# Two macaron blocks on one core: rings of q and k for the first two head groups moved into the pool beside the feed-forward, and chunk 1's q and k prepared there

## The chip, the cores and the metric

The kernel runs on one core of a Trainium2 chip. Its five engines work side by side, each on its own queue of instructions in program order: TensorE (PE; PEld is its loading of weights), VectorE (DVE), ScalarE (ACT), GpSimd (POOL) and SyncE (SP), which here issues nearly all DMA transfers. Engines wait for one another through semaphores. The metric is the time of one execution on the device in microseconds (us); lower is better. Times of the kernel before are the median of three runs and one execution with the profiler on.

## What is computed

One sequence of S = 2048 tokens with E = 256 features passes through two blocks. Each block is feed-forward (halved), attention, feed-forward (halved), each on a layernorm of x and added to x:

```python
x = x + 0.5 * _L0_ffn_ref(_layernorm(x), w_gate_up, w_proj)      # f0
x = x + _L0_attn_ref(_layernorm(x), W_qkv, W_o)                  # layer 0
x = x + 0.5 * _L0_ffn_ref(_layernorm(x), w_gate_up, w_proj)      # f1
x = x + 0.5 * _L1_ffn_ref(_layernorm(x), w_gate, w_up, w_down)   # f2
x = x + _L1_attn_ref(_layernorm(x), Wq, bq, Wk, bk, Wv, bv, Wo, bo)   # layer 1
x = x + 0.5 * _L1_ffn_ref(_layernorm(x), w_gate, w_up, w_down)   # f3
```

Both attentions are causal with 16 heads of 16 features. Layer 0 adds a slope per head times the distance (ALiBi); layer 1 adds biases and turns q and k by a rotary embedding (rope). The layer 0 feed-forward has ternary weights, silu(gate) times up over 1024 hidden features, and an RMS norm ahead of the second product. The layer 1 feed-forward keeps, of each four hidden features, the two that are largest in size.

## The kernel before

x stays in SBUF transposed (features on partitions) in four chunks of 512 tokens. A feed-forward goes chunk by chunk, eight steps f each: gate and up matmuls (pg, L306 and L281), silu on ACT (L317), the product on DVE (L318), and, per chunk, the second matmul (po, L361 and L292), part of which runs during the next chunk's steps. For the last chunk po stands alone at the end. Layernorms of chunks already done run piece by piece in between (`pull`); `pending[c]` counts those of chunk c still under way, and `ready(c)` draws them to their end.

Instructions on PE, ACT, DVE and POOL stay in the order in which the Python code issues them. Work is interleaved by generators: each `yield` hands the turn back. `attention(layer, following)` is such a generator. Its first value is the generator `first()`, which prepares chunk 0 beside the end of the feed-forward ahead of the attention: `beside0` and `beside1` begin it once the room is free, and `go_on` draws one step of it per f in the second half of the third chunk and in the fourth, two per f in the fourth chunk if the weights of layer 1 are loaded, as they are ahead of layer 1. `attend()` draws what is left of it after the feed-forward, and then the rest of the attention. What `first()` uses lies in pool `ka`, opened beside the feed-forward on the other side of SBUF. All else of the attention lies in pools `kv` and `at` (L640 to L642), opened when the feed-forward's pool is closed, so that their tiles take over its room and wait for its last readers.

Preparation of a chunk c:

- `prep_qk(c, what)` (L533 on): two pairs of matmuls (pp, L548; four instructions each, one step per pair). In layer 0 ACT casts the first bf16 piece (L556) and DVE subtracts it (L557). In layer 1 ACT adds the bias (L559); two DMAs copy the halves of dn swapped into sw (L568); a DVE multiply by the cosine (L583), a POOL multiply by the sine (L587) and a DVE add (L589) do the rope, and a cast and a subtraction (L593) give the first piece. Two more pieces follow on ACT (L595) and POOL (L596). The three pieces, which make up an fp32 value, are written to scratch in DRAM, dk or dq, with six DMAs (L601). The pieces' tiles have one buffer each; dn has two in layer 0 and one in layer 1; sw and cs have one.
- `prep_v(c)` (L607 on): two steps of eight matmuls (pv, L613), then copies into va.

`load(n, kc)` reads back the k of chunk kc for group n (four heads; n = 4 c + g), and q of group n once: one DMA of 384 KB from dk or dq (L655) and one of constant rows (L660) for each. The tiles are rings in `kv`: four of k of the group's own chunk (kd), five of k of earlier chunks (ko), four of q. SP issues these in order with all else on it.

Scores are computed twice. First for the maxima: `mx_unit` makes, for each of four heads, a score matmul (pq, L686), a mask matmul (L694), and a DVE reduce out of PSUM (mx, L697); the scores take turns in three PSUM buffers (`ps_one`), which pp, pv and others share. `mx_end` makes the negated maximum of a group in three pieces (neg, L704 and L709), `mx_turn` turns it (ptm, L719; qx on ACT, L727) and three DMAs put it into q's tile as rows (L729). Then, for every block of 128 keys, `st_pair` makes the transposed scores (pst, L748, mask L756), ACT the exponential (pT, L768) and PE the product with v (pav, L783); DVE and POOL divide (L804 to L809), and the output matmul (L824) follows.

At the attention's start there are seven units of maxima ahead of the first exponential: the four of group 0 (`maxima[-1]`, widths 128 to 512 tokens), and three of group 1. Between them `step()` draws the preparation of chunk 1 from `preps`, one step per unit in layer 0, two in layer 1:

```python
load_to(-1)
preps.extend((prep_qk(1, "k"), prep_qk(1, "q"), prep_v(1)))
for unit in maxima[-1]:
    mx_next(unit, (0, 1, 2, 3))
    for _ in range(1 + layer):
        step()
```

`load_to(i)` issues the loads of all units due by slot i; `need(...)` draws `preps` on until a piece that is wanted is there. The last unit of group 1 stands between score matmuls of the first exponential.

## Time and profile before

| what | value |
|---|---|
| median of 3 runs | 1911.72 us (1908.17, 1911.72, 1911.8) |
| profiled execution | 1911.92 us |
| its span | 1910.1 us |
| mean granted PE clock | 0.971 |
| PE busy | 1728.1 us, 90% |
| DVE busy | 1354.6 us, 71% |
| ACT busy | 892.9 us, 47% |
| POOL busy | 415.3 us, 22% |
| chain that ended last | PE 70%, DVE 18%, ACT 3%, issue 3%, POOL 3%, DMA 1% |

The span is the stretch from the first to the last instruction that the profiler recorded; the time of the execution is 1.8 us longer. The chain is found by going back from the last instruction to what released it, and so on; an engine's share there says how much of the span hung on it. The granted clock is the share of full speed that PE was allowed. In timelines the bracket at the end of a row gives how long the engine had been idle before it, and whose end released it.

### The profile page before, as it was taken

The numbers are of one execution on the slowest core, as the hardware profiler recorded it, in microseconds if no ns is written. First come the engines' busy times: TensorE is split into PE (matmuls) and PEld (weight loads), VectorE is DVE, ScalarE is ACT, GpSimd is POOL, SyncE is SP. The second block draws the span as 40 slices with busy tenths as digits, with TensorE's granted clock in tenths as the row PEclk, the third lists the DMA queues.
The fourth block names the chain that finished last, engine by engine and source line by source line (L and its number), as shares of the span: only waits on it lengthen the run. The fifth ranks groups of instructions, "written<-read, shape, count | busy, mean of one in ns | idle before, by whom it ended". The sixth has DMA issues, their size and how long they took to land.

```text
span 1910.1 us, 27066 instructions
## 1 busy us (share of the span) xinstructions
PE 1728.1 (90%) x10684; PEld 743.0 (39%) x10684; DVE 1354.6 (71%) x2400; ACT 892.9 (47%) x1158; POOL 415.3 (22%) x386
## 2 busy tenths in 40 slices
PE   5699788999999999888999995889999999998999
PEld 1234343443444443333434442434334444433443
DVE  7867368787788884467666674878877888825665
ACT  4244143555556667433442222545555556673221
POOL 3456321110000000246532332212101000004100
PEclk9799899999999999989999997999999999999999
DMA  4001143312211000200000025313112210000000
GB/s 132 1 1 61 52 130 83 103 47 79 88 56 47 28 28 1 75 1 0 1 12 0 11 89 157 106 55 115 53 46 73 84 44 27 18 2 0 11 11 22
DMA packets 50512, 93.11 MB, mean 49 GB/s; under 512 B 5425, under 2 KB 33073, under 8 KB 50129
## 3 DMA queue, kind: packets, MB, share of 16 engines
q1 hardware_dynamic: 49296, 89.28, 15.3%
q10 hardware_dynamic: 1088, 2.10, 0.3%
q8 instruction: 84, 1.38, 0.3%
q14 instruction: 44, 0.35, 0.1%
HBM read 59.51 MB, written 27.26 MB: 45 GB/s over the span
## 4 chain that ended last, share of the span: by engine, by line
PE 70%; DVE 18%; ACT 3%; issue 3%; POOL 3%; DMA 1%; SPq 0%; DVEq 0%; ACTq 0%; POOLq 0%
PE pav L783 14%; PE pst L748 11%; PE pq L686 10%; PE pg_f L281 8%; DVE mx L697 8%; PE pg_f L306 6%; PE po_f L292 6%; PE po_f L361 4%; PE pp_q L548 2%; PE pp_k L548 2%; PE pwo L824 2%; PE pv L613 1%; PE pst L756 1%; PE pq L694 1%; DVE h_f L329 1%
## 5 line engine op out<-in xcount | busy, mean ns | idle before, releaser
L697 DVE TENSOR_REDUCE mx<-pq 128x1 f32<-128x512 f32 (+3 forms) x1280 | 697.1, 602 | 145.8 <-PE pq L694 81.5
L768 ACT ACTIVATE pT<-pst 128x1024 f32<-128x1024 f32 (+3 forms) x616 | 536.4, 897 | 332.4 <-PE pst L748 171.5
L686 PE MATMUL pq<-k,q 105*128 105x512 bf16 (+7 forms) x1280 | 386.6, 350 | 72.7 <-DVE mx L697 49.0
L748 PE MATMUL pst<-q,k 99*128 99x512 bf16 (+7 forms) x1280 | 355.8, 352 | 10.4 <-ACT pT L768 6.6
L783 PE MATMUL pav<-pT,va 128*32 128x256 f32 (+1 forms) x4608 | 324.3, 377 | 5.5 <-DVE yt L804 5.0
L281 PE MATMUL pg_f<-xn,wgu 128*128 128x512 f32 x512 | 229.1, 598 | 11.9 <-DVE hr_f L318 11.8
L809 POOL TENSOR_TENSOR zt<-yt,rd 128x64 f32<-128x64 f32 x128 | 41.3, 322 | 811.4 <-DVE rd L808 807.0
L748 PEld LDWEIGHTS <-k 105*128 105x128 bf16 (+1 forms) x1280 | 111.1, 98 | 230.0 <-issue 165.9
L686 PEld LDWEIGHTS <-q 105*128 105x128 bf16 (+1 forms) x1280 | 123.3, 99 | 146.6 <-issue 45.2
L783 PEld LDWEIGHTS pav<-pT,va 128*32 128x32 f32 x4608 | 106.2, 108 | 189.5 <-issue 134.8
L306 PE MATMUL pg_f<-xn,wgu 128*128 128x512 bf16 x512 | 154.8, 410 | 19.1 <-DVE wgu L170 6.8
L317 ACT ACTIVATE sl_f<-pg_f 128x512 f32<-128x512 f32 x128 | 75.9, 593 | 172.2 <-PE pg_f L281 97.3
L281 PEld LDWEIGHTS pg_f<-xn,wgu 128*128 128x128 f32 x512 | 97.0, 191 | 138.9 <-issue 114.5
L306 PEld LDWEIGHTS <-wgu 128*128 128x128 bf16 x768 | 77.2, 101 | 162.6 <-issue 69.0
L340 POOL TENSOR_TENSOR ss_f<-ss_f,sq_f 128x512 f32<-128x512 f32 x56 | 90.6, 1617 | 112.4 <-ACT sq_f L339 107.9
L292 PE MATMUL po_f<-h_f,wd 128*128 128x512 f32 x256 | 112.1, 592 | 0.0
L694 PE MATMUL pq<-mask_qk,ident_b 128*128 128x128 bf16 x512 | 106.2, 224 | 0.0
L756 PE MATMUL pst<-mask_kq,ident_b 128*128 128x128 bf16 x512 | 102.8, 221 | 0.0
L318 DVE TENSOR_TENSOR h_f<-sl_f,pg_f 128x512 f32<-128x512 f32 x64 | 43.6, 681 | 78.7 <-ACT sl_f L317 78.5
L804 DVE STREAM_TRANSPOSE yt<-pav 128x128 f32<-128x128 f32 x128 | 39.9, 311 | 78.1 <-PE pav L783 78.1
L306 PE MATMUL pg_f<-xm_f,wgu 128*128 128x512 bf16 x256 | 84.4, 412 | 11.9 <-DVE xm_f L238 11.9
L318 DVE TENSOR_TENSOR hr_f<-sl_f,pg_f 128x512 f32<-128x512 f32 x64 | 43.7, 683 | 64.0 <-ACT sl_f L317 63.9
(132 smaller groups left out, 1787.3 us busy)
## 6 DMA issues: line engine op xcount, KB each, us to landing
k<-dk SPq DMA_DIRECT2D x80, 384.0 KB
dk<-p_k SPq DMA_DIRECT2D x48, 256.0 KB
dq<-p_q SPq DMA_DIRECT2D x48, 256.0 KB
q<-dq SPq DMA_DIRECT2D x32, 384.0 KB
x<-in_xT ACTq DMA_DIRECT2D x4, 512.0 KB
raw<-in_w_gu SPq DMA_DIRECT2D x8, 256.0 KB
wgu<-in_w_gu SPq DMA_DIRECT2D x1, 2048.0 KB
cs_k<-in_cos_sin SPq DMA_DIRECT2D x4, 512.0 KB
```

Source lines behind the costliest of these rows:

```text
L281: nc.tensor.matmul(pg[:, half, :], lhsT=wgu[:, dc, half * F + f * P : half * F + (f + 1) * P], rhs=xn[:, dc, :], start=dc == 0, stop=dc == ...
L292: nc.tensor.matmul(po, lhsT=w[:, f, dc * P : (dc + 1) * P], rhs=h[:, f, :], start=f == 0, stop=f == FC - 1,)
L306: nc.tensor.matmul(pg[:, half, :], lhsT=wgu0[:, dc, half * F + f * P : half * F + (f + 1) * P], rhs=xp[part][:, dc, :], start=part == 0 an ...
L318: nc.vector.tensor_tensor(to, sl, pg[:, 1, :], ALU.mult)
L340: nc.gpsimd.tensor_tensor(ss, ss, sq, ALU.add)
L686: nc.tensor.matmul(pq, lhsT=qs[n][0:rows, hh, t * P : (t + 1) * P], rhs=ks[n, kc][0:rows, hh, 0:w], start=True, stop=kc < c,)
L694: nc.tensor.matmul(pq[:, w - P : w], lhsT=ident_b, rhs=mask_qk, start=False, stop=True)
L697: nc.vector.tensor_reduce(mxs[n][:, t, hh, kc : kc + 1], pq, AX.X, ALU.max)
L748: nc.tensor.matmul(ps[i][:, lo:CH], lhsT=ks[n, kc][0:rows, hh, t * P : (t + 1) * P], rhs=qs[n][0:rows, hh, lo:CH], start=True, stop=kc < c,)
L756: nc.tensor.matmul(ps[i][:, lo : lo + P], lhsT=ident_b, rhs=mask_kq, start=False, stop=True)
L768: nc.scalar.activation(pT[:, :, lo:CH], pair[:, :, lo:CH], AF.Exp, scale=0.25)
L783: nc.tensor.matmul(acc[hh * SLOT : (hh + 1) * SLOT, a:b], lhsT=va[kc][:, t, v0 : v0 + SLOT], rhs=pTs[hh // 2][:, hh % 2, a:b], start=kb == ...
```

## The change

The rings are split by group. Groups whose number modulo 4 is 0 or 1 have their k of the own chunk and their q in pool `ka`, two buffers each; groups 2 and 3 have theirs in `kv`, two buffers each; all k of earlier chunks stay in `kv`, five buffers. Before `kv` is open, `ring` can only give `ka`. `first()` now also issues the loads of groups 0 and 1 for chunk 0 (after q and after v of chunk 0 are prepared), then notes "first" as done, waits until the layernorm of chunk 1 has been asked for (and, while `kv` isn't open, until it is finished), and goes on with k and q of chunk 1. What of this is not done when the feed-forward ends is drawn by `step()` in the attention, with v of chunk 1 behind it. `go_on` draws two steps per f in the fourth chunk ahead of layer 0 as well, and ahead of layer 1 already in the second half of the third; in the maxima's loop there is one step per unit in either layer. The memsets of va of chunks 1 to 3 are issued together when `kv` opens, and no longer by each chunk's preparation of k.

```diff
     def layernorm(c, name):
 
         pending[c] += 1
+        asked.add(name)
...
-    def attention(layer, following):
+    def attention(layer, before, following):
...
                 ready(c)
-                if what == "k" and c > 0:
-                    nc.gpsimd.memset(va[c], 1.0)
...
-            yield first()
-            kv = st.enter_context(tc.tile_pool(name=f"kv{layer}", bufs=1))
-            ap = st.enter_context(tc.tile_pool(name=f"at{layer}", bufs=2))
-            va += [values(kv, c) for c in range(1, NCH)]
...
+            pools = [ka]
 
             qs = {}
             ks = {}
+
+            def ring(n, other=False):
+
+                return pools[0 if other or n % 4 > 1 else -1]
...
-                need("k", kc)
-                ks[n, kc] = kv.tile(
-                    [P, 4, CH], BF16, tag="kd" if kc == c else "ko", bufs=4 if kc == c else 5,
+                ks[n, kc] = ring(n, kc < c).tile(
+                    [P, 4, CH], BF16, tag="kd" if kc == c else "ko", bufs=2 if kc == c else 5,
                     name=f"k{layer}_{n}_{kc}",
                 )
...
                 if n not in qs:
-                    need("q", c)
-                    qs[n] = kv.tile([P, 4, CH], BF16, tag="q", bufs=4, name=f"q{layer}_{n}")
+                    qs[n] = ring(n).tile([P, 4, CH], BF16, tag="q", bufs=2, name=f"q{layer}_{n}")
                     stack(qs[n], "q", c, a["q_rows"][g])
+
+            def first():
+                nc.gpsimd.memset(va[0], 1.0)
+                yield
+                for work in (prep_qk(0, "k"), prep_qk(0, "q")):
+                    yield from work
+                load(0, 0)
+                yield from prep_v(0)
+                load(1, 0)
+                done.add("first")
+                while f"after_{before}_1" not in asked or len(pools) == 1 and pending[1]:
+                    yield
+                for work in (prep_qk(1, "k"), prep_qk(1, "q")):
+                    yield from work
+
+            beginning = first()
+            yield beginning, done
+            kv = st.enter_context(tc.tile_pool(name=f"kv{layer}", bufs=1))
+            ap = st.enter_context(tc.tile_pool(name=f"at{layer}", bufs=2))
+            pools.insert(0, kv)
+            va += [values(kv, c) for c in range(1, NCH)]
+            for c in range(1, NCH):
+                nc.gpsimd.memset(va[c], 1.0)
...
                 while uses and uses[0][1] <= slot:
-                    load(*uses.popleft()[0])
+                    (n, kc), _ = uses.popleft()
+                    if (n, kc) not in ks:
+                        need("k", kc)
+                        need("q", n // G)
+                        load(n, kc)
 
             load_to(-1)
-            preps.extend((prep_qk(1, "k"), prep_qk(1, "q"), prep_v(1)))
+            preps.extend((beginning, prep_v(1)))
             for unit in maxima[-1]:
                 mx_next(unit, (0, 1, 2, 3))
-                for _ in range(1 + layer):
-                    step()
+                step()
...
         if at == NCH - 1 or at == NCH - 2 and f >= FC // 2:
             next(begun[1], None)
-            if w1 and at == NCH - 1:
+            if w1 or at == NCH - 1:
                 next(begun[1], None)
...
     def attend():
-        att, first = begun
-        for _ in first:
-            pass
+        att, first, done = begun
+        while "first" not in done:
+            next(first)
         next(att, None)
         begun.clear()
```

More of the change, by code (lines that the diff above doesn't have):

```diff
@@ L185, in macaron_kernel @@
     pending = [0] * NCH
+    asked = set()
     def draw(work):
@@ L631, in prep_v @@
                     yield
-            def first():
-                nc.gpsimd.memset(va[0], 1.0)
-                yield
-                for work in (prep_qk(0, "k"), prep_qk(0, "q"), prep_v(0)):
-                    yield from work
-            yield first()
-            kv = st.enter_context(tc.tile_pool(name=f"kv{layer}", bufs=1))
-            ap = st.enter_context(tc.tile_pool(name=f"at{layer}", bufs=2))
-            va += [values(kv, c) for c in range(1, NCH)]
-            acc = ps_acc(f"pav{layer}")
-            zts = {}
-            zs = {}
+            pools = [ka]
             qs = {}
             ks = {}
+            def ring(n, other=False):
+                return pools[0 if other or n % 4 > 1 else -1]
             def load(n, kc):
@@ L668, in load @@
                 if n not in qs:
-                    need("q", c)
-                    qs[n] = kv.tile([P, 4, CH], BF16, tag="q", bufs=4, name=f"q{layer}_{n}")
+                    qs[n] = ring(n).tile([P, 4, CH], BF16, tag="q", bufs=2, name=f"q{layer}_{n}")
                     stack(qs[n], "q", c, a["q_rows"][g])
+            def first():
[19 more added lines that the diff above has]
+                nc.gpsimd.memset(va[c], 1.0)
+            acc = ps_acc(f"pav{layer}")
+            zts = {}
+            zs = {}
             mxs = {}
@@ L1036, in macaron_kernel, with begin @@
     begun = []
-    def begin(layer, following):
-        att = attention(layer, following)
-        begun[:] = att, next(att)
+    def begin(layer, before, following):
+        att = attention(layer, before, following)
+        begun[:] = att, *next(att)
     def go_on(at, f):
@@ L1050, in beside0 @@
             raw_scope.close()
-            begin(0, "f1")
+            begin(0, "f0", "f1")
         go_on(at, f)
@@ L1057, in beside1 @@
             ffn0_scope.close()
-            begin(1, "f3")
+            begin(1, "f2", "f3")
         if s == 1:
```

## The prediction

> **What bounds the kernel now.** The page first: PE is busy 90% of 1910.1 us, and the chain of work that ended last is 70% PE, 18% DVE, 1% DMA. So PE time counts nearly everywhere, and the change must earn its time where PE stands still. Cutting the span into stretches of 10 us finds such places where each attention begins (columns: stretch, length, busy us of PE, PEld, DVE, ACT, POOL with counts, granted PE clock, DMA share, GB/s):
> ```profile
> 230.00:240.00 10.00, 4.44 (x12) 2.10 (x13) 0.98 (x4) 0.00 (x0) 0.57 (x1) 0.56 0.89 244
> 240.00:250.00 10.00, 7.89 (x31) 3.70 (x30) 6.96 (x14) 2.22 (x3) 2.12 (x1) 0.84 0.44 143
> ...
> 1160.00:1170.00 10.00, 3.75 (x16) 1.58 (x14) 6.18 (x11) 1.04 (x1) 3.53 (x2) 0.65 0.66 173
> ...
> 1180.00:1190.00 10.00, 5.10 (x26) 2.76 (x26) 4.92 (x11) 0.51 (x1) 3.53 (x2) 0.68 0.54 135
> ```
> In the first, DMA is 0.89 busy and the rest idle; in all four the clock is low. PE's timeline there says why (start, duration; brackets: idle before, and releaser):
> ```profile
> 235.53 0.27 PE L686 MATMUL pq<-k,q 105*128 105x128 bf16 x1 [8.22 <-DMA q<-in_q_rows]
> ...
> 236.56 3.78 PE L548 MATMUL pp_k<-xn,wqkv 128*128 128x512 f32 x4
> ...
> 242.40 1.99 PE L548 MATMUL pp_k<-xn,wqkv 128*128 128x512 f32 x4
> ...
> 248.84 3.38 PE L548 MATMUL pp_q<-xn,wqkv 128*128 128x512 f32 x4
> ...
> 1152.87 0.27 PE L686 MATMUL pq<-k,q 99*128 99x128 bf16 x1 [6.37 <-DMA q<-in_q_rows]
> ...
> 1165.65 0.48 PE L686 MATMUL pq<-k,q 99*128 99x384 bf16 x1 [4.62 <-DVE mx L697]
> ...
> 1186.06 0.27 PE L686 MATMUL pq<-k,q 99*128 99x128 bf16 x1 [4.56 <-DVE mx L697]
> ```
> Two waits for the read-back of q and k (8.22 and 6.37 us), then, in layer 1, two waits in which DVE, PE's releaser, itself stands at a rope multiply until the swapped halves land:
> ```profile
> 1163.91 1.23 DVE L583 TENSOR_TENSOR dn_k<-dn_k,cs_k 128x1024 f32<-128x1024 f32 x1 [3.31 <-DMA sw_k<-dn_k]
> ...
> 1184.58 1.22 DVE L583 TENSOR_TENSOR dn_q<-dn_q,cs_k 128x1024 f32<-128x1024 f32 x1 [3.41 <-DMA sw_q<-dn_q]
> ```
> The same projection beside a feed-forward, in PE's timeline, runs at full clock: 1.71 us to the next matmul's start at 157.66.
> ```profile
> 155.95 1.88 PE L548 MATMUL pp_k<-xn,wqkv 128*128 128x512 f32 x4
> ```
>
> **How I sum.** Against the profiled run: 1911.92 us, span 1910.1 and 1.8 around it; 0.2 from the median of 1911.72. In each layer I measure one stretch, from the end of the feed-forward's last po_f matmul to the last neg of the second group (L709); behind it both programs hold nearly the same work in the same order (read from the order of instructions of the two built programs). Before: layer 0 from 227.3 to 265.7, **38.4 us**; layer 1 from 1146.5 to 1192.4, **45.9**. What the change adds beside the feed-forward is counted into the new stretch.
>
> **Layer 0.** By the built order all four pairs of chunk 1's k and q matmuls move into the last feed-forward chunk, between gate/up matmuls, and the reads k_0, q_0, k_1, q_1 are issued there. Step by step:
> - Beside the feed-forward PE gets 4 x 1.72 = 6.9 us, and I add 0.3 for a PSUM buffer not free at once: 7.2. Casts (4 x 0.57 and 2 x 1.03 us ACT) and subtractions (4 x 0.69 DVE) cost nothing: in 200 to 210 us DVE is busy 5.43 of 10, ACT 4.08. Uncovered, the DVE part would cost 2.8.
> - The load wait goes. Next late is the feed-forward's residual add on POOL (L370, ends 229.46), which still frees the room that the maxima tiles take: 2.2 after po_f. Before, the reads were issued only behind it.
> - From there DVE sets the pace. First group's reduces, four of 128, 256, 384 and 512 wide, by rows: 1.04 + 1.41 + 1.94 + 2.48 = 6.9. Its neg 0.6. Second group: 1.94 + 1.41 + 1.04 = 4.4, then 2.5 with 0.3 ahead of it for the score matmuls, neg 0.6.
> - v of chunk 1 stays, 1.99 us of PE in each of two pieces. Three PSUM buffers of scores cover some 0.5 of each: gaps of 1.5 and 1.4. The turn of the first group leaves 0.7 (0.39 PE, 0.57 ACT, less the queued reduces).
> - Sum: 7.2 + 2.2 + 6.9 + 0.6 + 4.4 + 0.3 + 2.5 + 0.6 + 2.9 + 0.7 = 28.3. **Gain 10.1**.
> - The three memsets at opening (3 x 1.05 us POOL, by the row of one) stand ahead of nothing due in 3 us: 0. Four more reads of 384 KB (k of groups 4 to 7) now go to SP ahead of the rows q<-qx of group 1. Reads of this size move at 244 GB/s in the row above, 1.6 us each; the rows are due behind some 5 us of work: 0 to 3 us, taken 0.
>
> **Layer 1.** Only k's matmuls, biases and rope of chunk 1 get into the feed-forward; the casts of k and all of q remain.
> - Beside the feed-forward: 2 x 1.72 = 3.4. The tile dn is single there, so ACT's bias of chunk 0's q waits for POOL's last read of k, which today costs PE 2.57 us (gate/up at 1096.43 waits for DVE hr_f); with twice the steps the chain closes up, I take 3.0: +0.4. Rope's two DVE steps, 2 x 1.23, go between the sparsity selects; DVE ends 4.3 us ahead of the last po_f today, which hides them. If DVE waits there for the swapped halves, up to 5.
> - Residual add on DVE, 0.75, takes the place of the load wait.
> - DVE: reduces 6.9, neg 0.6, k's subtraction (L593) 1.2, second group 4.4, gap at the second q matmuls 1.1, at the turn 0.9. Then rope's multiply of q: its halves land 4.5 us after issue (1159.45 to 1163.91), with 2.4 us of reduces between: wait 2.4, multiply 1.2. Then 2.4 and neg 0.6. Sum 21.7.
> - Owed behind the stretch: q's add (L589), 1.2.
> - 3.4 + 0.4 + 0.75 + 21.7 + 1.2 = 27.5. **Gain 18.4**: one wait for swapped halves instead of two, no load wait, one projection pair at a full clock instead of a low one.
>
> **Clock.** The trace has no such stretch without a wait. Nearest rows: after idles of 8.22, 6.37 and 4.62 us the matmuls run slow (3.78 instead of 1.99), after 2.57 at 1093.9 they don't (next gate/up eight 3.70, others 3.60). The new stretches idle in bits of under 2.5 us, so mostly full clock; but 10 us at half PE load may be seen as idle. A low clock costs 1.7 us a pair. Bounds: none, or two pairs in each layer, 6.8. I take half a pair in layer 0 (0.8) and one in layer 1 (1.7), nearer to the row with the small gap. The Trainium skill ("TensorE: Matmul & The Clock Gate", Part 1, A second HAM failure mode) has the clock halved after an idle window of about 3.4 us, and also by many small idles between groups of matmuls that cycle through PSUM. The first agrees with these rows; by the second the sum would be rival A.
>
> **Sum**: 1911.9 - 10.1 - 18.4 + 0.8 + 1.7 = **1886**.
>
> **Rivals.**
> - A. The wait is only replaced: PE, short of work behind DVE, stays at the low clock, and the wait for q's halves grows. All four pairs slow, 4 x 1.7 - 2.5 taken = 4.3, and q's wait back at 4.6 instead of 2.4, 2.2: **1892**. For it: 0.65 to 0.68 in layer 1 now; against: those stretches hold 4.6 us idles.
> - B. Moving the projections brings nothing, since feed-forward and maxima are both paced by PE and DVE; only the load waits go: 8.22 - 2.2 and 6.37 - 0.75, 11.6: **1900**. This is also what is left if chunk 1's preparation falls behind as before. Against: the built order, and 3.78 against 1.71 us a pair.
> - C. Slower. The pieces of k and q (part0 to part2) have one buffer each. Four preparations now follow one another in the last chunk, so ACT's cast of the next must wait until the writes of the last have landed, with the feed-forward's silu behind it on ACT, and PE behind silu. Six writes of 256 KB took 7.46 and 9.52 us of issue at 166 and 181. Five such waits; each has about 4 us of other ACT work and buffered gate/up tiles for cover. It decides if a landing comes some 10 us later than this cover, at five places: 50 - 26 = 24 us slower, **1936**. Break-even lies at 5.2 us each. Against: before, the same sequence k, q of chunk 0 shows no PE wait for it in layer 0.
> - D. The rows q<-qx late behind the four reads, or DVE waiting for swapped halves inside the feed-forward: 1 to 5 us, up to **1891**.
>
> **Chances.** Forecast with D 0.55, A 0.20, B 0.15, C 0.07; 0.03 for an accident near no change. Measurements of this kernel tell about 0.2%, 3.8 us, from no change. Faster 0.90, same 0.03, slower 0.07. Low end: full clock (-2.5), no wait for q's halves (-2.4), the 3.0 stall gone, q's add hidden (-1.2): 1877, with the sum's rounding 1876. High end: B, 1900. The range leaves out C and a part of B.
>
> **What would show it.** Layer 0: the first pq released by POOL or DVE, not by q_rows, within 2.5 us; pp_k and pp_q between pg_f at 1.9 us; stretch po_f to neg near 21 + 0.8. Layer 1: no 6.37, one of the two 4.6 waits, about 2.4; pp_q alone behind pq; stretch 22.5 + 1.7. Clock near 1.0 in layer 0's first 20 us, under 0.8 would be A. Gate/up waiting for ACT or DVE by more than 5 us in the last chunk would be C. I am wrong by most if the moved work meets a queue that I took for free: SP beside the feed-forward, or DVE between the selects.

## The result, and the profile after

The changed kernel takes **1901.0 us** (median of 5 runs, 1895.57 to 1901.93). The kernel before, run beside it, takes 1911.72 (median of 5, 1908.17 to 1915.95). The ratio is **0.994 [0.9922, 0.9958]**: faster, by 8 to 15 us. The forecast was 1886 in 1876 to 1900; the gain of the profiled run is 10.0 us (1911.92 to 1901.93) where 25.9 were expected.

The stretches at the head of both attentions got shorter, as forecast. Timeline of the kernel after in stretches, columns as in the prediction (layer 0's head is 238.7 to 262.2, layer 1's 1150.6 to 1175.0):

```profile
240.00:250.00 10.00, 7.60 (x42) 5.16 (x41) 5.73 (x15) 1.29 (x4) 5.02 (x5) 1.00 0.67 173
250.00:260.00 10.00, 7.91 (x42) 4.51 (x43) 7.09 (x19) 3.13 (x4) 0.00 (x0) 0.69 0.36 104
...
1160.00:1170.00 10.00, 8.86 (x48) 4.11 (x47) 4.31 (x12) 4.64 (x6) 0.00 (x0) 0.91 0.39 95
1170.00:1180.00 10.00, 7.07 (x32) 3.47 (x32) 7.63 (x15) 3.49 (x5) 3.82 (x3) 0.60 0.44 115
```

No slice has PE at 4 or 5 of 10 any more, but two of these four still have a low clock. PE's timeline of the kernel after (L701 is the score matmul that was L686, L548 the projection; a bracket is the idle time before and its releaser):

```profile
239.47 0.22 PE L701 MATMUL pq<-k,q 105*128 105x128 bf16 x1 [0.62 <-DVE y_f L371]
...
241.13 0.22 PE L701 MATMUL pq<-k,q 105*128 105x128 bf16 x1 [1.39 <-DVE mx L712]
...
1157.75 3.78 PE L548 MATMUL pp_q<-xn,wqkv 128*128 128x512 f32 x4
...
1172.58 0.58 PE L701 MATMUL pq<-k,q 99*128 99x512 bf16 x1 [2.85 <-DVE mx L712]
```

The waits of 8.22 and 6.37 us for the read-back are gone: what is late next is the residual add of the feed-forward (y_f, x), for which PE stands 0.6 us in either layer. In layer 0 DVE's first reduce waits for POOL's part of it as well, until 240.79, 2.2 us behind the last po_f as forecast; that is the 1.39 us at 241.13. Only q's pair is left in layer 1, and one wait for swapped halves, 2.85 us at PE, which DVE's timeline shows as 2.57:

```profile
1170.70 1.23 DVE L583 TENSOR_TENSOR dn_q<-dn_q,cs_k 128x1024 f32<-128x1024 f32 x1 [2.57 <-DMA sw_q<-dn_q]
```

On the page of the kernel after, PE is busy 1732.2 us (91%) and DVE 1362.7 (72%), in a span of 1900.1 at a clock of 0.970; of the chain 71% is PE and 19% DVE, one per cent more each. So where did the rest of the gain go? I compare both profiles by the same points: the end of each feed-forward (its last residual add), the second neg, the first output matmul's add to x behind it, and the first residual add of the next layer's part (for layer 0 that of f2). A stretch is taken here from the start of the last residual add, up to 0.1 us behind the end of po_f. All in us, plus is later:

| | forecast | measured |
|---|---|---|
| layer 0: feed-forward ahead ends later | 7.2 | 11.3 (1.0 of it with rings alone too) |
| its stretch, last po_f to second neg | 38.4 to 21.9 | 38.25 to 23.48 |
| from there to the first add of the output (82.59 before) | 0 | -1.2 |
| **layer 0 together** | **-9.3** | **-4.7** |
| layer 1: feed-forward ahead ends later | 3.8 | 8.8 |
| its stretch | 45.9 to 24.15 | 45.89 to 24.36 |
| from there to the first add (86.62 before) | +1.2 | +6.4 |
| further on | 0 | +1.1 |
| **layer 1 together** | **-16.7** | **-5.2** |

The stretches are right to 1.6 and 0.2 us. The feed-forwards cost 9 us more than forecast, and 6 us come back late, behind layer 1's stretch.

### The profile page after: what moved, and what is told of

It reads as the page before. It is cut to its first block, busy times and chain, and to the rows that moved or that the text cites. A ratio compares the mean times of both kernels' runs of the same rounds, so it can differ in the third digit from the quotient of the medians.

```text
span 1900.1 us, 27042 instructions
## 1 busy us (share of the span) xinstructions
PE 1732.2 (91%) x10658; PEld 744.5 (39%) x10684; DVE 1362.7 (72%) x2400; ACT 892.3 (47%) x1158; POOL 419.8 (22%) x386
## 3 DMA queue, kind: packets, MB, share of 16 engines
q8 instruction: 84, 1.38, 0.3%
## 4 chain that ended last, share of the span: by engine, by line
PE 71%; DVE 19%; ACT 3%; issue 3%; POOL 3%; DMA 1%; SPq 0%; DVEq 0%; ACTq 0%; POOLq 0%
PE pav L798 14%; PE pst L763 12%; PE pq L701 11%; PE pg_f L283 8%; DVE mx L712 7%; PE pg_f L308 6%; PE po_f L294 5%; PE po_f L363 4%; PE pp_k L548 2%; PE pwo L839 2%; PE pv L613 1%; PE pp_q L548 1%; PE pst L771 1%; PE pq L709 1%; DVE h_f L331 1%
## 5 line engine op out<-in xcount | busy, mean ns | idle before, releaser
L701 PE MATMUL pq<-k,q 105*128 105x512 bf16 (+7 forms) x1280 | 389.5, 353 | 48.3 <-DVE mx L712 41.5
L701 PEld LDWEIGHTS <-q 105*128 105x128 bf16 (+1 forms) x1280 | 124.0, 99 | 132.2 <-issue 31.3
```

What stands on the lines that cost most here:

```text
L701: nc.tensor.matmul(pq, lhsT=qs[n][0:rows, hh, t * P : (t + 1) * P], rhs=ks[n, kc][0:rows, hh, 0:w], start=True, stop=kc < c,)
```

## The experiments

**My theory** after the result: (T1) PE and DVE time that is moved beside a feed-forward is paid there in full, and more; (T2) the maxima at an attention's head hide most of such work once the data are there in time; so the early loads do everything and moving the preparation does nothing or harm. **Its rival**: the moved preparation is worth what the forecast said, and is eaten by something that can be mended (a POOL operation in the wrong place, a late q, a low clock). All kernels in one table; ratios are to the kernel before, run beside each of them (medians 1911.7 to 1914.28):

| run | us | ratio [95%] |
|---|---|---|
| a1_layer0_alone | 1907.72 | 0.9981 [0.9963, 0.9999] |
| a2_layer1_alone | 1907.73 | 0.9976 [0.9966, 0.9986] |
| a3_rings_alone | 1895.24 | 0.9914 [0.9892, 0.9935] |
| a4_prep_alone | 1920.24 | 1.0033 [1.0018, 1.0047] |
| b1_extra_pe | 1903.33 | 0.9947 [0.993, 0.9964] |
| b2_last_piece_dve | 1900.49 | 0.994 [0.9923, 0.9956] |
| b3_rings_one_step | **1890.46** | 0.9886 [0.9871, 0.9901] |
| b4_two_steps | 1902.05 | 0.9946 [0.9925, 0.9967] |
| c1_prep_alone | 1912.1 | 0.9996 [0.9982, 1.0009] |
| c3_v_in_maxima | 1895.8 | 0.9917 [0.9895, 0.9939] |
| c4_v_between | 1896.54 | 0.9911 [0.9892, 0.9931] |
| d1_longer_gap | 1893.16 | 0.9893 [0.9877, 0.991] |
| d2_pe_beside_ffn | 1911.81 | 0.999 [0.9978, 1.0002] |
| e1_norm_on_dve | 1893.01 | 0.991 [0.9881, 0.9939] |
| e2_little_pe | 1896.3 | 0.9907 [0.9884, 0.9931] |
| f1_rings_little_pe | 1892.81 | 0.989 [0.9872, 0.9907] |

One caution for all that follows. The kernel after, e1, e2 and b4 have the same code up to the end of layer 0, yet in their four profiles layer 0 gains 4.7, 13.4, 4.5 and 5.2 us, with a granted clock in its stretch of 0.85 (23.48 us) in the first and 0.92 (21.78 us) in e1. A single profile tells a layer's gain to several us only. I take totals from the medians, and from profiles only rows and numbers that repeat.

### The change taken apart: one layer, one part

Two flags per layer: EARLY puts the rings in `ka` and issues the loads in `first()`; PREP lets `first()` go on with chunk 1.

```diff
+EARLY = (True, True)      # per layer
+PREP = (False, False)
...
-                load(0, 0)
+                if EARLY[layer]:
+                    load(0, 0)
...
+                if not PREP[layer]:
+                    return
...
-            preps.extend((beginning, prep_v(1)))
+            if PREP[layer]:
+                preps.extend((beginning, prep_v(1)))
+            else:
+                preps.extend((prep_qk(1, "k"), prep_qk(1, "q"), prep_v(1)))
...
-                step()
+                for _ in range(1 if PREP[layer] else 1 + layer):
+                    step()
```

a1 and a2 do both parts in one layer, a3 the rings in both, a4 the preparation in both.

> The change in layer 0 alone; layer 1 keeps its rings, waits and order of before. Theory 'paid elsewhere' (most of what the maxima's stretch gained was paid beside the feed-forward and, in layer 1, behind the stretch): aligned anchors of the two traces give layer 0 a net gain of 5.5 us, so 1906. Rival 'layer 1 undoes it' (layer 0 kept its forecast 9.3 and layer 1 lost the rest or nearly nothing was gained there): 1902.

> The change in layer 1 alone. Theory 'paid elsewhere': net gain 4.2 us, 1907.5; the stretch from the feed-forward's last po_f to the second neg about 14 us better than before after paying about 9 beside the feed-forward, and about 9 given back between group 2 and the end of chunk 1. Rival 'the giving back has to do with layer 0's part': gain about 14 here, 1898.

> Early loads of groups 0 and 1 alone: rings in the pool beside the feed-forward, chunk 1's k and q prepared in the attention as before. Theory 'paid elsewhere': load waits of 8.2 and 6.4 fall to 2.2 and 0.8, nothing is added beside the feed-forward, so about 11.6 better: 1900, as good as the whole change, so that moving the preparation is worth about nothing. Rival 'the parts need each other' (without the moved preparation the maxima stay as slow as before and the load wait only turns into another wait): gain under 6, 1906 or more.

> Chunk 1's preparation beside the feed-forward alone; all loads issued when the attention's pools open, as before. Theory 'paid elsewhere': the load waits of 8.2 and 6.4 are back, so the net gains of 5.5 and 4.2 turn into losses of about 0.5 and 1.4: 1912 to 1914. Rival 'the moved preparation is what gained': 1901 plus no more than the waits not hidden, 1905.

**a3, the rings alone, gain 16 us** (12 to 21 by the interval): more than the whole change. Each layer alone, with both parts, is worth 4 us. In a1 and a4 I had by oversight left layer 0's preparation at two steps per f in the second half of the third chunk too, which the change does not do; there its feed-forward ends 16.7 and 17.9 us late. So c1 does a4 again at the change's pace:

> Chunk 1's preparation beside the feed-forward alone, with loads at the attention's start as before, and now at exactly the changed kernel's pace (two steps a step f ahead of layer 0 in the fourth chunk only). Theory 'PE work is dear beside the feed-forward and cheap in the maxima': no gain, 1911 to 1916. Rival 'the preparation gained by itself, the earlier run at a quicker pace hid it': 1905 or less.

It takes 1912.1 us, **0.9996 [0.9982, 1.0009]**: moving the preparation alone brings nothing. Why the rings alone do so much is seen in a3's timeline in layer 0's maxima, where the projections have stayed (L550 here):

```profile
231.03 1.99 PE L550 MATMUL pp_k<-xn,wqkv 128*128 128x512 f32 x4
...
241.51 1.98 PE L550 MATMUL pp_q<-xn,wqkv 128*128 128x512 f32 x4 [0.17 <-DVE mx L718]
```

Each pair takes 1.99 us where the kernel before had 3.78 and 3.38. The low clock was made by the load wait, and goes with it. The whole stretch, cut out of a3's timeline, has clock 1.00:

```profile
228.43:256.95 28.52, 22.05 (x107) 11.77 (x105) 17.55 (x43) 8.76 (x12) 8.55 (x6) 1.00 0.59 178
```

28.52 us with all four pairs in it, and the feed-forward is no later than 1.0. The forecast for the full change was 21.9 here plus 7.2 in the feed-forward, 29.1. Even with its own numbers the second part was worth nothing on top of the first in layer 0; I had priced what it removes at a clock that the first part had already mended. In layer 1 a3's stretch is still 39.73 us long, with two waits for swapped halves; there it takes another pace (b3, below) to be as short without the move.

### What work beside the feed-forward costs, and why it is more than its own time

d2 takes b3 (below) and adds matmuls that nothing waits for beside the end of both feed-forwards, of the size of the projections. b2 gives the last subtraction of the pieces (L596) to DVE for chunk 1 in layer 0.

```diff
+        if at == NCH - 1 and 2 <= f < 6:                # d2; layer 1: 4 < f < 7
+            useless(f"no0_{f}", attn_w[0][0])           # 4 matmuls of 128x512 f32
...
-                nc.gpsimd.tensor_tensor(pt[2], dn, pt[1], ALU.subtract)      # b2
+                last = nc.vector if layer == 0 and c == 1 else nc.gpsimd
+                last.tensor_tensor(pt[2], dn, pt[1], ALU.subtract)
```

> Early loads with one step per unit (1890.5), with useless PE work beside the feed-forward alone: in the last chunk ahead of layer 0 four groups of four fp32 matmuls of 512 columns (what chunk 1's k and q take of PE), ahead of layer 1 two groups, written to PSUM and never read; no ACT, DVE, POOL or DMA work comes with them. It prices PE time by itself there. Theory 'PE bounds the feed-forward': 6.9 and 3.4 us longer at the feed-forwards' ends, so that of the 10.5 and 8.8 that the change cost there 3.6 and 5.4 are side effects (POOL beside DVE, the single dn, the clock); total 1900 to 1901. Rival 'there is slack, and the side work is what cost': under 4 and 2, total 1893 to 1896.

> The changed kernel, but in layer 0 the last subtraction of chunk 1's k and q (L596) goes to DVE in place of POOL. Theory 'POOL slows DVE at the feed-forward's end': in the profile after, two DVE steps of 0.7 us took 2.2 and 1.8 beside it and the last wait of PE for ss was 7.8 in place of 5.1; with DVE doing it (1.2 us) that wait falls to about 6.0 to 6.5 and the time by 1.5 to 2.5 us, to 1899. Rival 'that wait comes from the moved layernorm and casts on ACT': wait stays above 7, time within 1 us of 1901.

In d2's timeline of PE each group of four is recorded as eight, two records per fp32 instruction, and so the added time was twice what I had written (a pair of the projections, x4 in the rows, is only two instructions), and the total of 1911.81 misses both forecasts:

```profile
185.61 3.60 PE L1098 MATMUL no<-xn,wqkv 128*128 128x512 f32 x8
```

At 3.43 us to the next matmul, that is 4 x 3.43 = 13.7 us in layer 0 and 6.9 in layer 1. The feed-forwards end 13.6 and 6.8 us later than b3's. **PE time beside a feed-forward costs 0.99 us per us**, as the forecast had it (4 x 1.72 and 2 x 1.72). But the moved preparation costs 8.7 to 8.8 us in layer 1 in seven profiles of kernels with it (after, a2, b1, b2, b4, c1, e1; 10.1 in e2, of which 1.5 lie in f1, ahead of the moved work) instead of 3.4, and in layer 0 9.1 to 11.3 instead of 6.9. The rest isn't PE's own time. In layer 1, PE's timeline of the kernel after:

```profile
1087.83 3.70 PE L283 MATMUL pg_f<-xn,wgu 128*128 128x512 f32 x8 [1.28 <-DVE hr_f L320]
...
1095.94 4.54 PE L283 MATMUL pg_f<-xn,wgu 128*128 128x512 f32 x6 [3.33 <-DVE hr_f L320]
...
1143.18 1.12 PE L294 MATMUL po_f<-h_f,wd 128*128 128x512 f32 x2 [0.63 <-DVE h_f L428]
```

Two stalls, 4.6 us where before there was one of 2.57; behind the second the matmuls run slow, 0.76 us each instead of 0.46; and a bit at the end, where DVE comes late to the h_f that PE needs, since its step ahead of it (L422, 1140.57) took 1.83 us beside POOL's rope multiply (1137.59 to 1141.59), where the same step took 0.96 in the kernel before. The cause of the second, longer stall is in ACT's timeline:

```profile
1093.99 0.69 ACT L559 ACTIVATE dn_q<-pp_q,b_qk 128x512 f32<-128x512 f32 x1 [3.06 <-POOL p_k L596]
```

ACT waits for POOL to be done with dn, and silu stands behind it. That is the term I had put at 0.4, as a small growth of the 2.57 us. But those 2.57 us are no wait for dn. In PE's and DVE's timelines of the kernel before:

```profile
1096.43 3.70 PE L281 MATMUL pg_f<-xn,wgu 128*128 128x512 f32 x8 [2.57 <-DVE hr_f L318]
```

```profile
1091.11 2.28 DVE L583 TENSOR_TENSOR dn_k<-dn_k,cs_k 128x1024 f32<-128x1024 f32 x1
1094.55 1.22 DVE L589 TENSOR_TENSOR dn_k<-dn_k,sw_k 128x1024 f32<-128x1024 f32 x1 [1.16 <-POOL sw_k L587]
1095.69 0.68 DVE L318 TENSOR_TENSOR hr_f<-sl_f,pg_f 128x512 f32<-128x512 f32 x1
```

The hr_f that PE needs stands on DVE behind the rope of chunk 0's k. ACT's wait for dn came later there (2.24 us, until 1105.90), while PE had the second matmul to do, and cost PE nothing; at twice the pace it comes ahead of a silu that PE needs. 2.0 (idle) + 1.8 (six slow matmuls) + 0.6 make 4.4 of the 5.4 us.

In layer 0 what grows is the wait for the RMS sum: PE stands 7.82 us for POOL's ss_f at 223.68, where the kernel before stands 5.13 and d2, with more PE work but none for POOL, 5.14. That is 2.7 of the 4.4 us beyond PE's own time. DVE's and POOL's timelines of the kernel after say why:

```profile
213.86 2.22 DVE L336 TENSOR_TENSOR hm_f<-h_f 128x512 f32<-128x512 f32 x1
216.00 1.78 DVE L331 TENSOR_TENSOR h_f<-hm_f 128x512 bf16<-128x512 f32 x1
...
221.21 0.69 DVE L336 TENSOR_TENSOR hm_f<-h_f 128x512 f32<-128x512 f32 x1
```

```profile
213.40 2.13 POOL L596 TENSOR_TENSOR p_q<-dn_q,p_q 128x1024 bf16<-128x1024 f32 x1
215.49 1.70 POOL L342 TENSOR_TENSOR ss_f<-ss_f,sq_f 128x512 f32<-128x512 f32 x1
```

The same DVE product takes 0.69 us alone and 2.22 beside POOL's subtraction. It ends at 216.08, 0.55 behind POOL's 215.53: as if it had stood still until POOL was done. The Trainium skill ("SBUF — State Buffer", SBUF: two separate sides) says just that: of a GpSimd operation and a DVE operation with two SBUF inputs, the one that starts first holds the shared ports for its whole length. These rows agree within 0.2 us. b2 takes L596 off POOL: the wait becomes 6.52 and the feed-forward ends 8.0 late instead of 11.3. The total doesn't move (1900.49): 1.8 of these 3.3 us come back in layer 0's stretch (25.23 us at a clock of 0.73 instead of 23.48 at 0.85). The wait is as the theory had it, the total as the rival had it.

### How much the maxima hide

b1 adds six score matmuls with a useless result to each unit of the maxima of the changed kernel, where nothing waits for them:

```diff
                 mx_next(unit, (0, 1, 2, 3))
+                for _ in range(6):
+                    nc.tensor.matmul(acc, lhsT=qs[0][0:RM, 0, 0:P],
+                                     rhs=ks[0, 0][0:RM, 0, :], start=True, stop=True)
```

> The changed kernel with useless work added: after each of the seven units of maxima at an attention's start, six score matmuls of 512 columns into the accumulator that the first product with v overwrites (about 1.3 us a unit at full clock). It adds PE work and changes no result. Theory 'clock' (the stretch from which the projections were taken runs at a low clock because PE now idles there): the clock stays near 1.0 in both stretches, the extra work hides behind DVE's reduces, and the time falls by 1 to 4 us, to 1897 to 1900. Rival 'only order and work count': the extra work lies partly in the open, 0.3 to 0.6 us a unit, 1905 to 1909.

1903.33, against 1901.0. Rows of b1, the two stretches (237.1 on and 1151.8 on):

```profile
237.13:264.85 27.72, 23.44 (x142) 13.55 (x140) 15.45 (x40) 6.45 (x9) 5.53 (x5) 1.00 0.52 140
...
1151.77:1178.20 26.43, 23.52 (x140) 12.38 (x138) 17.63 (x42) 7.33 (x9) 8.70 (x6) 1.00 0.58 158
```

The same rows of the kernel after are 23.48 us at clock 0.85 and 24.36 at 0.80. Some 9 us of added work per layer (7 units of 6 matmuls at 0.22 us) made the stretches 4.2 and 2.1 us longer: **0.2 to 0.5 us per us** (0.65 in layer 0 if e1's profile of the same code, 21.78, is taken), where a feed-forward takes 0.99. That is T2, with half of its reason: PE's gaps there are filled, and with them filled the clock is 1.00 in both stretches. The forecast's term for a low clock was thus real; its size b1 doesn't show, since the added work covers it.

But it holds for work that nothing waits for. c3 moves real work in: v of chunk 0 out of the feed-forward into layer 1's and layer 0's maxima of b3; c4 instead moves it, in layer 1, between k and q in `first()`.

```diff
-                yield from prep_v(0)                                      # c3
...
-                preps.extend((prep_qk(1, "k"), prep_qk(1, "q"), prep_v(1)))
+                preps.extend((prep_v(0), prep_qk(1, "k"), prep_qk(1, "q"), prep_v(1)))
...
-                for work in (prep_qk(0, "k"), prep_qk(0, "q")):           # c4
+                between = [prep_v(0)] if layer == 1 else []
+                for work in (prep_qk(0, "k"), *between, prep_qk(0, "q")):
```

> Early loads with one step per unit, and PE work moved the other way: chunk 0's v (two pieces, 3.4 us of PE in each layer) leaves the feed-forward and is prepared between the units of maxima ahead of chunk 1's k. In the run with useless score matmuls 9.2 us of added PE work cost 2 to 3 us a layer, a price of about 0.3 us per us; beside the feed-forward the price is 1.0 or more. Theory: 3.4 us saved against 1 to 2 paid in each layer, 2 to 5 us better than 1890.5: 1886 to 1888. Rival 'the maxima are as full as the feed-forward once the loads are early': 1890 to 1893.

> Early loads with one step per unit; in layer 1 chunk 0's v is prepared between its k and q. ACT's bias of q then no longer waits for POOL's last read of the single tile dn, for which PE stood 2.57 us. Theory: this idle goes and nothing else moves, 2 to 3 us better than 1890.5: 1888. Rival: q of chunk 0 gets ready 10 us later, so its read comes back to the head of the attention: 1891 to 1894.

Both miss: 1895.8 and 1896.54, 5 to 6 us above b3, with intervals that just overlap. c4 was built on the same misreading: with q out of the way the idle that it was to remove is still there, 2.56 us at 1086.35, since it is not dn's. Its feed-forward ends 5.6 us late in layer 1: the eight matmuls behind that idle take 5.39 us instead of 3.70, PE stands another 1.94 us for DVE's h_f at 1133.18, and sixteen matmuls behind that take 8.83 instead of 7.03. Behind its stretch are 98.05 us. c3's feed-forwards end earlier than b3's, by 4.3 and 1.5 us, and its stretches grow by 3.6 (28.53 to 32.09) and 0.7, and 4.8 behind (92.77 to 97.55): 9.1 given back for 5.8. So T2 as I had put it, that the maxima hide any work, falls. They hide PE work without a follower; a preparation there brings its casts and adds to a DVE and ACT on which PE waits. This last reason fits the rows, and no run isolates it.

### What comes back behind layer 1's stretch

Behind layer 1's stretch the kernel after takes 93.00 us where before took 86.62. Rows of before and of after:

```profile
1192.43:1279.05 86.62, 74.50 (x610) 36.77 (x610) 68.71 (x161) 43.17 (x57) 18.93 (x27) 0.98 0.28 84
```

```profile
1174.95:1267.95 93.00, 80.93 (x603) 38.20 (x601) 71.07 (x162) 42.11 (x56) 18.90 (x26) 0.89 0.29 82
```

PE has about as many matmuls (603 and 610) and is busy 6.4 us longer with them, at a clock of 0.89 instead of 0.98. The same 0.89 stands in a2 (92.73 us), b2 (92.80) and c1 (92.87). New work behind the stretch is only what I had named, q's add (L589, at 1174.87 after, 1188.18 before), 1.2 us; q's further pieces and v of chunk 1 stood behind it in the kernel before too. In slices, the kernel after has the clock fall again and again:

```profile
1175.00:1185.00 10.00, 9.65 (x73) 4.77 (x72) 7.02 (x15) 4.74 (x7) 2.02 (x3) 0.64 0.25 82
...
1205.00:1215.00 10.00, 7.79 (x41) 3.51 (x40) 8.20 (x18) 2.19 (x3) 2.90 (x4) 0.72 0.39 101
...
1225.00:1235.00 10.00, 8.35 (x58) 4.07 (x57) 8.86 (x20) 5.06 (x6) 3.08 (x4) 0.83 0.19 54
```

One of the falls can be followed. In PE's and DVE's timelines of the kernel after:

```profile
1208.49 0.32 PE L701 MATMUL pq<-k,q 99*128 99x384 bf16 x1 [1.95 <-DVE mx L712]
```

```profile
1206.08 1.48 DVE L724 TENSOR_TENSOR neg<-neg 128x16 f32<-128x16 f32 x2
```

neg, 0.38 us elsewhere (1159.14), takes 1.48 beside a layernorm step of POOL (L251, 1206.05 to 1207.31); PE stands 1.95 us for the reduces behind it, and the clock falls. Two theories: the low clock makes most of the 6.4 us, and fewer idles of PE win it back; or q's tail is paid there in any case, and a different pace only shifts it. e1 takes POOL's multiply (L271), which pushed L251 to that place, to DVE (it belongs to chunk 2's layernorm behind f2, not ahead of f3 as the expectation says); e2 adds 21 useless matmuls to layer 1's maxima, half of b1's dose; f1 adds the same to b3; b4 draws q's preparation at two steps per unit.

```diff
-                nc.gpsimd.tensor_tensor(xn[:, dc, :], xc[:, dc, :], sd, ALU.mult)   # e1
+                by = nc.vector if name == "after_f2_2" else nc.gpsimd
+                by.tensor_tensor(xn[:, dc, :], xc[:, dc, :], sd, ALU.mult)
...
+                for _ in range(3 * layer):          # e2, in the maxima; f1: the same on b3
+                    nc.tensor.matmul(acc, ...)
...
-                step()                              # b4
+                for _ in range(1 + layer):
+                    step()
```

> The changed kernel with two steps per unit in layer 1, as before the change. It tells what gave back 9.6 us behind the stretch in layer 1. Theory 'owed work' (the tail of q's preparation falls into the slots and pushes v and the layernorms behind it): the stretch gets longer by 2 to 4, the giving back falls to under 5, total 1896 to 1900. Rival 'clock and order of the layernorms': the giving back stays above 7 and the total is 1901 to 1906, since the wait for q's swapped halves grows again to 4.6.

> The changed kernel, but the last multiply of the layernorm of chunk 2 ahead of f3, which runs in layer 1's first slots, goes from POOL to DVE. Behind the stretch of layer 1 the change gave back 6.4 us, at a mean clock of 0.89 against 0.98 before. In the profile after, DVE's small step for the fourth group's negated maximum took 1.48 in place of 0.38 beside POOL at 1206, PE stood 1.95 us, and the clock was 0.68 in the 10 us from 1210. Theory 'clock, set off by single idles': without that collision the clock stays at 1.0 there and the part behind the stretch falls from 93.0 to 90 or less, total 1897 to 1899. Rival 'the tail of q's preparation costs that time, whatever the clock': it stays at 92 to 95 and the total at 1901 or more.

> The changed kernel with three useless score matmuls after each of the seven units of layer 1 only (0.7 us a unit, half the dose of the earlier run, whose stretch ran at full clock and came out 2.1 us longer for 9.2 us of added work). Theory 'clock': half the work keeps most of the clock, so that the stretch is no longer than the 24.4 of the changed kernel and the part behind it is shorter by 1 to 3, total 1898 to 1900. Rival: the work does not pay, stretch 25 to 26, total 1901 to 1904.

> Early loads with one step per unit (1890.5 with 4 runs), the best version so far, with the three useless score matmuls per unit of layer 1's stretch. There the clock was 0.81 over 26.4 us. Theory 'clock': it rises above 0.9, the stretch gets no longer and the total 1 to 3 us better, 1888. Rival 'here PE is busier with chunk 1's projections, so the added 4.6 us of work cost more than the clock brings': 1891 to 1893.

In e1's timeline neg has its 0.39 us again, and the clock stays up; the rows are its neg, one of PE, two slices, and all behind the stretch:

```profile
1198.93 0.39 DVE L725 TENSOR_TENSOR neg<-neg 128x16 f32<-128x16 f32 x2
```

```profile
1196.94 0.38 PE L702 MATMUL pq<-k,q 99*128 99x512 bf16 x1 [2.04 <-DVE mx L713]
```

```profile
1206.00:1216.00 10.00, 8.27 (x73) 3.75 (x66) 9.35 (x23) 4.08 (x6) 1.81 (x3) 1.00 0.42 122
1216.00:1226.00 10.00, 7.84 (x74) 4.16 (x76) 9.79 (x25) 6.22 (x8) 3.04 (x4) 1.00 0.00 2
...
1166.09:1254.75 88.66, 73.28 (x597) 35.72 (x596) 71.75 (x163) 41.79 (x55) 16.39 (x24) 0.96 0.29 86
```

88.66 us at 0.96; e2 has 90.26 at 0.94, b1 91.05 at 0.94. So among kernels with this work behind the stretch the length goes with the clock (0.89: 93.0; 0.94: 90.3 and 91.1; 0.96: 88.7; before, 0.98: 86.6), and all of them but the kernel before carry q's tail; e1 carries one more DVE step and is shorter still. That e1's edit kept the clock up is not shown, though. PE's idle only moved: it stands 2.04 us behind the multiply that DVE now does (the row at 1196.94), and there the clock doesn't fall (1.00 from 1196 to 1206). PE's idle of 1.38 us at 1229.10, behind which the clock of the kernel after fell to 0.83 in the slice, is in e1 too (1218.91), at 1.00. And in e1's stretch in layer 1, ahead of its edit, the clock is already 0.92 instead of 0.80. The same idle lowers the clock in one execution and not in another. Both medians lie under 1901.0 (1893.01 and 1896.3), but the intervals of their ratios overlap that of the kernel after, and e1's five runs go from 1888.64 to 1904.29. The rows speak for the clock; the medians don't prove it.

b4 decides nothing. It has 35.67 us at 0.76 in the stretch and 82.05 at 0.98 behind it, 117.7, where the kernel after has 24.36 + 93.00 = 117.4; its median is the same (1902.05). The tail of q costs as much in the one place as in the other, and a low clock is now in the stretch. f1 gains nothing over b3 (1892.81 against 1890.46): its stretch in layer 1 has 0.93 instead of 0.81, and is 26.17 us long instead of 26.39; behind it are 96.28 us instead of 92.77. So useless work is no remedy in itself.

### The version that beats both

b3 is a3 with one step per unit in layer 1 as well. d1 tries to win the same wait otherwise: on a3, two more steps between the bias and the rope multiply of chunk 1.

```diff
-                for _ in range(1 if PREP[layer] else 1 + layer):     # b3
+                for _ in range(1):
                     step()
...
-                    yield                                            # d1, on a3
-                    yield
+                    for _ in range(4 if c == 1 else 2):
+                        yield
```

> Early loads alone, with one step of chunk 1's preparation per unit in layer 1 in place of two. Theory: two steps put DVE's rope multiply only one unit behind its DMA, 4.5 us too early, and PE stood 5.7 and 4.6 us for it; with one step there are two units between, 3 to 5 us, so both waits fall under 2.5, but more of q is left for the slots: 1890 to 1893. Rival 'the preparation is merely pushed back and delays the slots or the loads of chunk 1': 1895 to 1900.

> Early loads alone (chunk 1 prepared in the attention, two steps per unit in layer 1), with four yields in place of two between the DMA of the swapped halves of chunk 1 and DVE's rope multiply. Theory 'the wait for the halves is what layer 1 loses in its stretch': DVE's two waits of 3.3 go, as with one step per unit, but less of q is left for the slots: 1887 to 1890. Rival 'what counts is the amount of preparation in the stretch': as with two steps, 1893 to 1896.

**b3 takes 1890.46 us, 0.9886 [0.9871, 0.9901]**, 22 us under before; its interval lies clear of the changed kernel's. The two differ in the move alone, since both have the early loads and one step per unit: with these in place, preparing chunk 1 beside the feed-forward costs 10 us. Against a3 (0.9914 [0.9892, 0.9935]) the intervals overlap, but the rows say what it wins. Layer 1's stretch and what is behind it, first of a3:

```profile
1139.66:1179.39 39.73, 23.03 (x92) 11.04 (x90) 22.25 (x45) 8.23 (x10) 12.16 (x8) 0.72 0.52 146
1179.39:1266.73 87.34, 75.23 (x610) 37.05 (x610) 68.70 (x161) 43.23 (x57) 17.92 (x26) 0.97 0.27 79
```

and of b3:

```profile
1138.08:1164.47 26.39, 18.83 (x98) 10.08 (x96) 21.64 (x43) 8.77 (x10) 8.64 (x6) 0.81 0.50 147
1164.47:1257.24 92.77, 78.06 (x604) 37.85 (x604) 70.89 (x163) 42.63 (x56) 21.26 (x28) 0.96 0.33 95
```

127.1 becomes 119.2. a3 still has the waits for swapped halves (PE stands 5.68 and 4.55 us for DVE); at half the pace the halves have landed when DVE's turn comes, and in b3's timeline the multiply of k has no bracket (nor has that of q, at 1181.38, behind the stretch):

```profile
1149.54 2.33 DVE L585 TENSOR_TENSOR dn_k<-dn_k,cs_k 128x1024 f32<-128x1024 f32 x1
```

(2.33 instead of 1.22 us, beside POOL's rope multiply, which began at 1149.53.) d1 buys time at the same place and comes to 1893.16, between a3 and b3.

## Why the prediction was wrong, point by point

The sum forecast 25.9 us and 10.0 were measured. Two of its terms make up the miss. What the moved work costs beside the feed-forwards was put at 7.2 and 3.8 us and measured at 11.3 and 8.8, 9 us more. What lies behind layer 1's stretch was put at 1.2 us and measured at 7.5, 6 us more. (The stretches came out 1.9 us longer, layer 0 behind its stretch 1.2 shorter.) Besides, the gain was credited to a part that brings none.

- **The load waits: right.** 8.22 and 6.37 us go, and the residual add is next. But their worth was mis-sized: rival B gave 11.6 us to them, a3 shows 16. The term left out is the low clock behind the wait, in the very rows I had quoted (3.78, 3.38).
- **The projections removed from the maxima as a source of gain: this step failed.** The stretch before holds them at that low clock, and I counted their going on top of the gain of the load waits. With early loads they cost 1.99 us a pair, at clock 1.00 and partly in PE's gaps. c1 shows 0.9996 for moving alone, b3 against after 10 us lost by it once the loads are early, and a3 in layer 0 28.52 us with the pairs against a forecast of 29.1 without.
- **7.2 and 3.8 us beside the feed-forward: too small by 3 and 5.** PE's part was right (d2: 0.99 us per us). Wrong were "casts and subtractions cost nothing" from a mean busy share of DVE, and +0.4 for the single dn. The 2.57 us wait was misread as dn's: it is DVE's, busy with the rope of chunk 0's k, and the wait for dn, which cost PE nothing before, came on top as 3.33 us with a slow clock behind it. POOL's subtraction wasn't priced at all; beside it a DVE step took 2.22 us for 0.69.
- **The stretches: right.** 23.5 and 24.4 us against 21.9 and 24.15; the wait for q's halves 2.57 against 2.4. The clock term of layer 1 (one slow pair, 1.7) is seen in the rows: behind the pair of 3.78 us DVE stands 2.79 us, until 1162.32, where 0.9 for the turn and 1.7 were forecast. In layer 0 it was put at 0.8, and the stretch is 2.4 us over the 21.1 without it, in e1's profile of the same code 0.7. The rule of micro-idles, which I gave less weight, did hold: the Trainium skill ("TensorE: Matmul & The Clock Gate", Part 1, A second HAM failure mode) has the clock go up and down when PE idles in small bits between groups of matmuls that cycle through PSUM. The trace agrees: here it fell behind an idle of 2.09 us at 251.85, with one of 2.85 at 1172.58, and at 1155 with none longer than 1.22 (from 1156 to 1160 it is 0.50).
- **"Behind it both programs hold nearly the same work in the same order": right of the work, wrong of its time.** 1.2 us of owed work were forecast there and 7.5 came. The work is the same, 603 matmuls for 610; they run at a clock of 0.89 instead of 0.98. The one fall followed above begins where PE waits for DVE. The clock was weighed in the stretch and not behind it.
- **The rivals.** The time is B's (1900), and so is its mechanism: moving the projections brings nothing. B even was too kind to them, since rings without the move are faster (b3 against after). A's low clock appeared in part, at A's places. C did not occur: the longest wait of gate/up in the last chunk is 3.33 us, and it is for dn, not for the DRAM writes. Of D, DVE's wait for swapped halves inside the feed-forward came to 0.73 us (at 1101.60).

**What stays open.** How much of the 7.5 us behind layer 1's stretch is the clock: the rows of e1 and e2 give it 3 to 4, and their intervals don't settle it. When exactly an idle lowers the clock: 2.57 us ahead of gate/up left eight matmuls at 3.70 in the kernel before, and the same 2.57 at the same place in a3 made them 5.40; e1's idles of 2.04 and 1.38 us above are another case.

```profile
1087.85 5.40 PE L285 MATMUL pg_f<-xn,wgu 128*128 128x512 f32 x8 [2.57 <-DVE hr_f L322]
```

And why the gains differ so from execution to execution (layer 0 of the same code: 4.7, 13.4, 4.5) beyond the clock rows given.

## What to carry to other kernels

Two parts of a change that mend the same stall must not both be paid with the stall's own rows: take one part away on paper and price the other at what is left, here the full clock of 1.99 us a pair instead of 3.78. Work moved beside the feed-forwards here cost its full PE time (0.99 us per us), and what its casts and subtractions did to ACT, DVE and POOL came on top; a stretch with gaps held useless work for 0.2 to 0.65. Before a wait is put down to a tile, follow it one step further than PE's releaser: what did that engine stand behind? Before a preparation is moved, try giving its transfers more time where it stands: in b3 one step per unit instead of two ended layer 1's waits for swapped halves.

## What the runs showed of the hardware

- With useless matmuls in the gaps the granted clock was higher: 1.00 in b1 instead of 0.85 and 0.80, for stretches 4.2 and 2.1 us longer with some 9 us of work each. That they pay is not shown: b1 takes 1903.33 and e2, with the smaller dose, 1896.3 against 1901.0, within overlapping intervals, and f1 nothing less than b3.
- A short idle can be paid for long. PE stood 2.09 us ahead of 251.85; in slices of 2 us the clock is then 0.94, 0.50, 0.50, 0.50, 0.85, with PE busy all along. In other executions the clock stayed at 1.00 behind such an idle (e1, 2.04 us at 1196.94).
- A short DVE step beside POOL takes POOL's time: 0.69 became 2.22 us, 0.73 became 1.78, two negs of 0.38 together became 1.48, and each ended within 0.6 us behind the POOL operation.
- One fp32 matmul instruction of the program is two matmuls in the records (d2's four gave x8, 3.60 us).
